# A two-layer block on one core: x through DRAM between stages, y summed by accumulating transfers, the feed-forward's activations split by GpSimd

## The chip, the cores and the metric

The kernel runs on one core of a Trainium2 chip. The metric is the device time of one execution in microseconds (us), median of three runs. The engines are TensorE (PE; its weight loads are PEld), VectorE (DVE), ScalarE (ACT), GpSimd (POOL) and SyncE (SP, which issues the transfers).

## The reference

Eight sequences of 512 tokens of width 256 pass through two layers, in float32. Each layer modulates a layernorm by per-sequence rows (`sa, ca, ga, sb, cb, gb`), adds a gated mixer and then a gated feed-forward. Cut to what matters:

```python
# layer 0: attention over features, then a shared and a routed feed-forward
h = layernorm(x) * (1 + ca) + sa
n = layernorm(h) * ln_g + ln_b
v, gate = split(silu(n @ W_hidden + b_hidden));  qk = silu(n @ W_qk + b_qk)
sim = einsum('bid,biD->bdD', qk * gamma0 + beta0, qk * gamma1 + beta1) / 512
x = x + ga * ((v * sum(softmax(sim), -1)[:, None] * gate) @ W_out + b_out + h)
h = layernorm(x) * (1 + cb) + sb
s = sigmoid(h @ router_w.T)          # the best 2 of 8 by s + bias, gates s / sum
x = x + gb * (silu(h @ sw1) * (h @ sw3) @ sw2 + sum_e comb_e * (gelu(h @ ew1[e]) @ ew2[e]))

# layer 1: a selective scan over time (512 channels, 16 states), then a ternary feed-forward
raw, gate = split(layernorm_mod(x) @ W_in)
h = silu(causal_conv4(raw));  ts, Bm, C = split(h @ W_x);  dt = softplus(ts @ W_dt + b_dt)
state[t] = exp(dt * A) * state[t - 1] + dt * Bm[t] * h[t]     # per channel and state d
y = sum_d state * C + h * D
x = x + ga * ((y * silu(gate)) @ W_out)
h = silu(tlin(x', w1)) * tlin(x', w2)          # tlin: ternary weights, then a scale per output
x = x + gb * tlin(gelu(tlin(gelu(tlin(h, h1)), h2)), w3)
```

## The kernel before

The work of one sequence (a "batch" b, eight in all) is four stages, each a Python generator that records operations: `front` (layer 0's mixer), `experts` (its feed-forward), `mixer` (the scan) and `ffn`. Activations lie with 128 tokens or 128 features on the partitions; most operations are 128x512 or 128x1024. Nothing is emitted while recording. Each operation carries its engine, an assumed cost, the buffers it reads and writes, and a due time: batch b's stage starts at b * TURN plus an offset, and a `lead` (RUSH, SLOW, EARLY) pulls an operation forward. `Plan.order` then plays a list scheduler over the assumed costs: at each moment an engine takes the ready operation with the earliest due time, if its buffers can be had from their pools, if it isn't more than AHEAD past the earliest open one, and (ScalarE) with LOOK added where the activation table would have to change. What comes out is one fixed order for each engine's queue, so a wait of one instruction holds up all that stand behind it on that engine.

Before all that, while the first batch's `front` runs, the kernel tests whether the feed-forward's weights are exact in the reduced format fp32r (`test`). With these inputs they are, and the branch that then runs multiplies in fp32r: an activation a is split into a high part rounded to fp32r and a low part a - high, and each weight meets both (`by`), so that a 128x512 product of one weight tile is two fp32r matmuls. Names used below:

- `st`, `v`, `decay`, `bp`, `crow`, `y`: the scan. For each state d and each half h of the channels (32 units u a batch) ScalarE writes exp(dt * A) to one of three `decay` buffers (L841), VectorE forms v = hs * B (L858) and scans 1024 wide over two chunks of 512 at once (L861; column 0 of each chunk of `decay` stays zero, which resets the state), GpSimd multiplies by C (L864) and adds to y (L866).
- `put` and the block after `gated`: the splits. ScalarE evaluates the activation twice, into the high part and back into PSUM (L991, L944), and VectorE subtracts (L915). For the first product of the feed-forward VectorE multiplies (L964), ScalarE casts (L971), VectorE subtracts (L973).
- `x_0` to `x_2`: x stays in SBUF from a batch's load to its `ffn`; three batches are held at once. `ffn` stores it to DRAM (`x_d`) and adds it back at the end through `xo`.
- `routing`: the scores take a sigmoid on ScalarE (L544), then some twenty small VectorE operations.
- matmul outputs: `ps_nT, ps_qk, ps_sim, ps_hv, ps_hg, pa_o` belong to front; `ps_hT, pg, pv, ps_r, pa_s, ps_e, pa_e` to experts; `ps_hTm, ps_raw, ps_x, ps_dt, ps_g, pa_m` to mixer; `ps_hTf, pg1, pv1, ps_h_s, pa_f, ps_o` to ffn (h1 and h2 are its two 1024x1024 products, a1 their first input).

## Time and profile before

| | us |
|---|---|
| median of 3 runs | 2246.09 (2244.88 to 2247.49) |
| the profiled execution, device time | 2246.68 |
| its span, first to last instruction | 2244.9 |
| busy in it: TensorE, ScalarE, VectorE, GpSimd | 1973.9, 1691.8, 1635.1, 1535.7 |
| mean granted TensorE clock | 0.94 of full speed |
| first product of the scan of batch 0, of batch 7 | 283.5, 1958.2 |
| last addition to y of batch 7, start | 2110.7 |

A row of the profile names the source line, the engine, the operation, the tiles written and read, the shapes and the count; then the busy time and the mean of one in ns; then how long the engine stood idle just before such instructions and who released it. The line of a matmul is that of a helper (L343), so matmuls are told apart by tiles. A window row gives busy time of each engine in a stretch of the execution. The span has a start of some 280 us in which the pipeline of batches fills, a middle that repeats every 243 us, and an end from 1958 on in which the last batch's scan and then its feed-forward run with little or nothing beside them.

### The profile page before, as it was taken

What the parts mean: (1) busy time and instruction counts of PE and PEld (TensorE: products, weight loads), DVE (VectorE), ACT (ScalarE), POOL (GpSimd) and SP (SyncE); (2) the same over time, 40 slices, a digit from 0 to 9 for tenths busy, and PEclk for the clock granted to TensorE, in tenths of its full rate; (3) what the DMA queues carried; (4) which work ended last, traced back from release to release, by engine and by line L of the source; (5) the groups of instructions that cost most, each with busy time, mean ns of one, the idle gap of its engine ahead of it and who ended that gap; (6) DMA issues with size and microseconds to landing.
All of it is one profiled execution on the core that took longest, in us unless ns stands there. A gap on an engine that the chain in (4) does not pass through costs nothing.

```text
span 2244.9 us, 22011 instructions
## 1 busy us (share of the span) xinstructions
PE 1973.9 (88%) x6916; PEld 1292.8 (58%) x6916; DVE 1635.1 (73%) x2074; ACT 1691.8 (75%) x2433; POOL 1535.7 (68%) x765
## 2 busy tenths in 40 slices
PE   1897879498999899999999999999999999768587
PEld 0455336245775567656765577656765677445465
DVE  4532589869885898669895998679876988598531
ACT  3522768569987898788988898789988898779442
POOL 1201488969896788567895789678876789399700
PEclk6998889699999999999999999999999999979888
DMA  9226335223453345334443345334533443335333
GB/s 264 77 93 191 88 108 167 79 91 122 142 175 106 112 133 171 112 111 139 158 157 117 115 150 174 116 118 140 170 121 117 140 150 116 120 108 169 103 104 105
DMA packets 186608, 294.52 MB, mean 131 GB/s; under 512 B 14232, under 2 KB 109728, under 8 KB 186480
## 3 DMA queue, kind: packets, MB, share of 16 engines
q1 hardware_dynamic: 186480, 293.01, 41.3%
q8 instruction: 57, 0.93, 0.2%
q14 instruction: 71, 0.58, 0.1%
HBM read 283.94 MB, written 20.55 MB: 136 GB/s over the span
## 4 chain that ended last, share of the span: by engine, by line
PE 67%; POOL 10%; ACT 9%; DVE 9%; issue 3%; DMA 1%; SPq 0%; DVEq 0%; POOLq 0%; ACTq 0%
PE ps_h_s L343 17%; PE pa_e L343 9%; PE ps_e L343 9%; PE ps_sim L343 4%; POOL st L864 4%; POOL y L866 4%; PE pg L343 4%; DVE st L861 3%; PE pv L343 3%; PE pa_m L343 3%; PE ps_qk L343 2%; PE pa_f L343 2%; PE ps_g L343 2%; PE pa_o L343 2%; PE pa_s L343 2%
## 5 line engine op out<-in xcount | busy, mean ns | idle before, releaser
L864 POOL TENSOR_TENSOR st<-st,crow 128x1024 f32<-128x1024 f32 x256 | 608.5, 2377 | 167.4 <-DVE st L861 103.0
L866 POOL TENSOR_TENSOR y<-y,st 128x1024 f32<-128x1024 f32 x256 | 607.7, 2374 | 18.1
L861 DVE TENSOR_TENSOR_SCAN st<-decay,v 128x1024 f32<-128x1024 f32 x256 | 584.6, 2284 | 35.7 <-POOL y L866 17.4
L841 ACT ACTIVATE decay<-dt,neg_a 128x511 f32<-128x511 f32 x512 | 335.8, 713 | 46.5 <-DVE st L861 41.3
L858 DVE TENSOR_TENSOR v<-hs,bp 128x1024 f32<-128x1024 f32 x256 | 313.3, 1224 | 13.6 <-ACT bp L853 8.6
L343 PE MATMUL ps_h_s<-a_h_sh,w_f_h 128*128 128x512 f32 x512 | 212.0, 414 | 35.3 <-DVE a_h_sl L915 31.7
L343 PE MATMUL ps_h_s<-a1h,w_f_h 128*128 128x512 f32 x512 | 220.5, 431 | 16.0 <-DVE a1l L973 14.7
L343 PE MATMUL pa_e<-w_e,ge 128*128 128x256 f32 x1024 | 232.1, 379 | 1.4 <-ACT ge L735 1.4
L343 PE MATMUL ps_e<-hT,w_e 128*128 128x512 f32 x512 | 231.4, 592 | 0.0
L343 PEld LDWEIGHTS pa_e<-w_e,ge 128*128 128x128 f32 x1024 | 194.4, 190 | 44.6 <-issue 15.3
L343 PE MATMUL ps_h_s<-a_h_sl,w_f_h 128*128 128x512 f32 x512 | 204.8, 400 | 0.0
L343 PE MATMUL ps_h_s<-a1l,w_f_h 128*128 128x512 f32 x512 | 202.8, 396 | 0.0
L841 ACT ACT_TABLE_LOAD x146 | 187.3, 1283 | 4.0 <-DVE st L861 1.3
L746 DVE SCALAR_TENSOR_TENSOR acc<-pa_e,rt,acc 128x256 f32<-128x256 f32 x256 | 112.0, 477 | 87.3 <-PE pa_e L343 86.3
L991 ACT ACTIVATE a_h_sh<-ps_h_s,cols 128x512 fp32r<-128x512 f32 x128 | 88.0, 688 | 110.4 <-PE ps_h_s L343 109.4
L915 DVE TENSOR_TENSOR a_h_sl<-ps_h_s,a_h_sh 128x512 fp32r<-128x512 f32 x128 | 87.4, 683 | 96.1 <-ACT ps_h_s L991 95.6
L343 PEld LDWEIGHTS ps_e<-hT,w_e 128*128 128x128 f32 x512 | 97.2, 190 | 92.4 <-issue 79.4
L343 PEld LDWEIGHTS ps_h_s<-a_h_sh,w_f_h 128*128 128x128 f32 x512 | 99.0, 193 | 70.4 <-DVE a_h_sl L915 35.7
L343 PEld LDWEIGHTS ps_h_s<-a1h,w_f_h 128*128 128x128 f32 x512 | 97.9, 191 | 48.9 <-DVE a1l L973 15.5
L735 ACT ACTIVATE ge<-ps_e 128x512 f32<-128x512 f32 x128 | 73.8, 598 | 54.1 <-PE ps_e L343 53.5
L343 PEld LDWEIGHTS ps_h_s<-a1l,w_f_h 128*128 128x128 f32 x512 | 97.9, 191 | 28.0 <-issue 8.7
L343 PE MATMUL ps_sim<-k,q 128*128 128x512 f32 x256 | 113.8, 603 | 0.0
(212 smaller groups left out, 3821.4 us busy)
## 6 DMA issues: line engine op xcount, KB each, us to landing
w_f_h<-fw_d SPq DMA_DIRECT2D x128, 512.0 KB, 3.5
w_e<-in_ew SPq DMA_DIRECT2D x128, 256.0 KB, 3.0
brow<-bc_d SPq DMA_DIRECT2D x128, 256.0 KB, 3.7
crow<-bc_d SPq DMA_DIRECT2D x128, 256.0 KB, 3.9
w_f<-fw_d SPq DMA_DIRECT2D x48, 512.0 KB, 4.0
w_s<-in_sw SPq DMA_DIRECT2D x24, 512.0 KB, 5.6
test<-in_f_h SPq DMA_DIRECT2D x16, 512.0 KB, 7.3
fw_d<-in_f_h SPq DMA_DIRECT2D x16, 512.0 KB, 6.4
```

The lines of the kernel that those rows point to most:

```text
L343: T.matmul(ps, lhsT=lhsT, rhs=rhs, start=(i == 0), stop=(i == last))
L735: op("ACT", 0.63, lambda ps=ps, g=ge[m]: A.activation(g.t, ps.t, AF.Gelu), r=[ps], w=[ge[m]], table="gelu", lead=RUSH)
L746: op("DVE", 0.48, lambda ps=ps, n=n, i=i, e=e: V.scalar_tensor_tensor(acc.t[:, n, :], ps.t[:, i * D : (i + 1) * D], comb(n, e), acc.t[:, n ...
L841: A.activation(decay[v % len(decay)].t[:, i, 1:], dt.t[:, c, 1:], AF.Exp, scale=neg_a.t[:, c, d : d + 1])
L858: op("DVE", 1.22, lambda v=v, cs=cs, bp=bp: V.tensor_tensor(v.t, hs.t[:, cs, :], over_tokens(bp.t, 2), ALU.mult), r=[hs, bp], w=[v])
L861: op("DVE", 2.28, lambda v=v, st=st, da=da: V.tensor_tensor_scan(st.t.rearrange("p c t -> p (c t)"), da.t.rearrange("p c t -> p (c t)"), v ...
L864: op("POOL", 2.4, lambda st=st, cc=cc: G.tensor_tensor(st.t, st.t, over_tokens(cc.t, 2), ALU.mult), r=[cc], w=[st])
L866: op("POOL", 2.4, lambda st=st, cs=cs: G.tensor_tensor(y.t[:, cs, :], y.t[:, cs, :], st.t, ALU.add), r=[st], w=[(y, pair(h))])
L915: op("DVE", 0.69, lambda: V.tensor_tensor(lo.t[:, at, :], ps.t, hi.t[:, at, :].bitcast(F32), ALU.subtract), r=[ps, (hi, at)], w=[(lo, at)] ...
L991: put(ps, nxt, m, lambda o, ps=ps, m=m, s=s: A.activation(o, ps.t, AF.Gelu, scale=col(s)[:, m : m + 1]), 0.69, [cols], table="gelu")
```

## The change

The scan: `decay` goes. ScalarE writes the exponentials straight into one of six `st` buffers, VectorE scans in place in two halves of 512, GpSimd multiplies by C, and y is summed by a transfer that GpSimd issues and that adds st to y. The feed-forward: an activation is evaluated once, into a float32 buffer (pool `two`, now six), and GpSimd makes the high part by a copy and the low part by a subtract (`split`). x: `experts` writes the new x to `x_d` in DRAM; `mixer` and `ffn` load it into `xn` and normalise it there, `mixer` loads it again in halves (`xm`), adds and stores it; two x buffers remain in SBUF. The router's sigmoid becomes exp, add and reciprocal. Four products reserve their results' buffers earlier (`need`). The planner's costs and due times change, with a separate turn for mixer and ffn; it also models the accumulating transfers, and lifts the AHEAD limit where nothing could be placed. The diff leaves out the planner's code and the `need` lines.

```diff
-TURN, FRONT, EXPERTS = 235.0, 64.0, 124.5
-MIX_AT, MIX = 221.7, 270.0
-FFN_AT, FFN = 531.0, 249.5
-FROM, UNTIL = 0.12, 0.949
-LOOK = 16.226
-DECAYS, BURST = 3, 1
-EARLY, RUSH, SLOW, AHEAD = 19.951, 14.0, 4.404, 69.662
+TURN, FRONT, EXPERTS = 206.087, 81.52, 133.488
+TURN_M, MIX_AT, MIX = 206.525, 229.452, 231.828
+TURN_F, FFN_AT, FFN = 208.187, 522.925, 195.397
+FROM, UNTIL = 0.218, 0.96
+LOOK = 38.649
+EARLY, RUSH, SLOW, AHEAD = 33.753, 17.315, -21.661, 137.531
...
-"two": (5, True), "bsc": (1, True), "bga": (1, True), "bgb": (1, True), "hs": (1, True),
-"dt": (1, True), "y": (1, True), "sp": (1, True), "st": (2, True), "bcb": (1, True),
+"two": (6, True), "bsc": (1, True), "bga": (1, True), "bgb": (1, True), "hs": (1, True),
+"dt": (1, True), "y": (1, True), "sp": (1, True), "st": (6, True), "bcb": (1, True),
...
-    op("ACT", 0.2, lambda: A.activation(at(SC, n), at(SC, n), AF.Sigmoid), w=[ps],
-       table="sigmoid", lead=RUSH)
+    op("ACT", 0.2, lambda: A.activation(at(SC, n), at(SC, n), AF.Exp, scale=-1.0), w=[ps],
+       table="exp", lead=RUSH)
+    v(0.2, lambda: V.tensor_scalar(at(SC, n), at(SC, n), 1.0, None, ALU.add))
+    v(0.2, lambda: V.reciprocal(at(SC, n), at(SC, n)))
...
-    op("POOL", 2.4, lambda: G.tensor_tensor(x.t, x.t, acc.t, ALU.add), r=[acc], w=[x], lead=RUSH)
-def mixer(b, x):
+    op("POOL", 2.4, lambda: G.tensor_tensor(acc.t, acc.t, x.t, ALU.add), r=[x], w=[acc], lead=RUSH)
+    op("SP", 1.7, lambda: SP.dma_start(out=x_d[b].t, in_=acc.t), r=[acc], w=[(x_d[b], (0, 1))], lat=2.0,
+       lead=RUSH)
+def mixer(b):
-    layernorm(x, xn, f"m{b}", RUSH)
+    load(xn, 512, lambda: SP.dma_start(out=xn.t, in_=x_d[b].t), r=[(x_d[b], (0, 1))])
+    layernorm(xn, xn, f"m{b}", RUSH)
...
-    def exps(u):
-        for v in range(u, u + BURST):
-            d, h = v // 2, v % 2
-            for i in range(2):
-                c = 2 * h + i
-                A.activation(decay[v % len(decay)].t[:, i, 1:], dt.t[:, c, 1:], AF.Exp,
-                             scale=neg_a.t[:, c, d : d + 1])
+    def exps(u, st):
+        d, h = u // 2, u % 2
+        for i in range(2):
+            c = 2 * h + i
+            A.activation(st.t[:, i, :], dt.t[:, c, :], AF.Exp, scale=neg_a.t[:, c, d : d + 1])
+    def scans(v, st):
+        for i in range(2):
+            V.tensor_tensor_scan(st.t[:, i, :], st.t[:, i, :], v.t[:, i, :], 0.0, ALU.mult, ALU.add)
-        da, cs = decay[u % len(decay)], slice(2 * h, 2 * h + 2)
+        cs = slice(2 * h, 2 * h + 2)
...
             op("ACT", 0.6, lambda bb=bb, bp=bp: A.copy(bp.t, bb.t), r=[bb], w=[bp], lead=SLOW)
-        if u % BURST == 0:
-            op("ACT", 1.42 * BURST, lambda u=u: exps(u), r=[dt, neg_a],
-               w=[decay[v % len(decay)] for v in range(u, u + BURST)], table="exp", lead=SLOW)
+        st = buf("st", [P, 2, S], f"st_{b}_{d}_{h}")
+        op("ACT", 1.42, lambda u=u, st=st: exps(u, st), r=[dt, neg_a], w=[st], table="exp", lead=SLOW)
-        st = buf("st", [P, 2, S], f"st_{b}_{d}_{h}")
-        op("DVE", 2.28, lambda v=v, st=st, da=da: V.tensor_tensor_scan(
-            st.t.rearrange("p c t -> p (c t)"), da.t.rearrange("p c t -> p (c t)"),
-            v.t.rearrange("p c t -> p (c t)"), 0.0, ALU.mult, ALU.add), r=[da, v], w=[st])
+        op("DVE", 2.35, lambda v=v, st=st: scans(v, st), r=[v], w=[st])
-        op("POOL", 2.4, lambda st=st, cs=cs: G.tensor_tensor(
-            y.t[:, cs, :], y.t[:, cs, :], st.t, ALU.add), r=[st], w=[(y, pair(h))])
+        op("POOL", 0.88, lambda st=st, cs=cs: G.dma_start(
+            out=y.t[:, cs, :], in_=st.t, accum_op=ALU.add), r=[st], w=[(y, pair(h))], move=2.8, lat=3.0)
...
-        add_gated(x, j, ps, ga, lambda: ga.t, f"tmpm_{b}_{j}")
-def ffn(b, x):
+        tmp, xo = buf("two", [P, 2, D], f"tmpm_{b}_{j}", line="tmp"), buf("two", [P, 2, D], f"xm_{b}_{j}", line="xm")
+        js = slice(2 * j, 2 * j + 2)
+        load(xo, 256, lambda xo=xo, js=js: SP.dma_start(out=xo.t, in_=x_d[b].t[:, js, :]),
+             r=[(x_d[b], j), (y, 0)], lead=RUSH, need=[tmp])
+        op("DVE", 0.69, lambda ps=ps, tmp=tmp: V.tensor_tensor(
+            tmp.t, ps.t.rearrange("p (i d) -> p i d", i=2), over_tokens(ga.t, 2), ALU.mult),
+            r=[ps, ga], w=[tmp], lead=RUSH)
+        op("POOL", 1.3, lambda tmp=tmp, xo=xo: G.tensor_tensor(tmp.t, tmp.t, xo.t, ALU.add),
+           r=[xo], w=[tmp], lead=RUSH)
+        op("SP", 1.4, lambda tmp=tmp, js=js: SP.dma_start(out=x_d[b].t[:, js, :], in_=tmp.t),
+           r=[tmp], w=[(x_d[b], j)], lat=2.0)
+def ffn(b):
     done, whole = 0.0, 80.0 if fast else 156.0
-    half = 0.5 if fast else 1.0
+    half = 0.53 if fast else 1.0
-    layernorm(x, xn, f"g{b}", RUSH)
-    op("SP", 2.7, lambda: SP.dma_start(out=x_d[b].t, in_=x.t), r=[x], w=[x_d[b]], lat=2.0)
+    load(xn, 512, lambda: SP.dma_start(out=xn.t, in_=x_d[b].t), r=[(x_d[b], (0, 1))])
+    layernorm(xn, xn, f"g{b}", RUSH)
...
-    def put(ps, a, k, fn, us, r, table=None):
-        hi, at = chunk(a, 0, k)
-        op("ACT", us, lambda: fn(hi.t[:, at, :]), r=[ps] + r, w=[(hi, at)], table=table, lead=RUSH)
+    def split(f, a, k):
+        (hi, at), (lo, _) = chunk(a, 0, k), chunk(a, 1, k)
+        op("POOL", 1.0, lambda: G.tensor_copy(hi.t[:, at, :], f.t), r=[f], w=[(hi, at)], lead=RUSH)
+        op("POOL", 1.3, lambda: G.tensor_tensor(
+            lo.t[:, at, :], f.t, hi.t[:, at, :].bitcast(F32), ALU.subtract),
+            r=[f, (hi, at)], w=[(lo, at)], lead=RUSH)
+    def put(ps, a, k, fn, us, r, name, table=None):
         if fast:
-            lo, _ = chunk(a, 1, k)
-            op("ACT", us, lambda: fn(ps.t), r=r, w=[ps], table=table, lead=RUSH)
-            op("DVE", 0.69, lambda: V.tensor_tensor(
-                lo.t[:, at, :], ps.t, hi.t[:, at, :].bitcast(F32), ALU.subtract),
-                r=[ps, (hi, at)], w=[(lo, at)], lead=RUSH)
+            f = buf("two", [P, S], name, line="split")
+            op("ACT", us, lambda: fn(f.t), r=[ps] + r, w=[f], table=table, lead=RUSH)
+            split(f, a, k)
+        else:
+            hi, at = chunk(a, 0, k)
+            op("ACT", us, lambda: fn(hi.t[:, at, :]), r=[ps] + r, w=[(hi, at)], table=table, lead=RUSH)
...
             if fast:
-                lo, _ = chunk(a, 1, m)
-                op("DVE", 0.745, lambda gated=gated, pv=pv: gated(pv.t), r=[sg, cols], w=[pv], lead=RUSH)
-                op("ACT", 0.62, lambda pv=pv, hi=hi, at=at: A.copy(hi.t[:, at, :], pv.t),
-                   r=[pv], w=[(hi, at)], lead=RUSH)
-                op("DVE", 0.69, lambda pv=pv, hi=hi, lo=lo, at=at: V.tensor_tensor(
-                    lo.t[:, at, :], pv.t, hi.t[:, at, :].bitcast(F32), ALU.subtract),
-                    r=[pv, (hi, at)], w=[(lo, at)], lead=RUSH)
+                f = buf("two", [P, S], f"f1_{b}_{m}", line="split")
+                op("DVE", 0.745, lambda gated=gated, f=f: gated(f.t), r=[pv, sg, cols], w=[f], lead=RUSH)
+                split(f, a, m)
...
-        load(xo, 256, lambda xo=xo, js=js: SP.dma_start(out=xo.t, in_=x_d[b].t[:, js, :]), r=[x_d[b]], lead=RUSH)
+        load(xo, 256, lambda xo=xo, js=js: SP.dma_start(out=xo.t, in_=x_d[b].t[:, js, :]),
+             r=[(x_d[b], j), fT[0]], lead=RUSH)
...
-slots_x = [fixed([P, NT, D], f"x_{i}") for i in range(3)]
-xs = [slots_x[b % 3] for b in range(B)]
+slots_x = [fixed([P, NT, D], f"x_{i}") for i in range(2)]
+xs = [slots_x[b % 2] for b in range(B)]
...
-    run(mixer(b, xs[b]), b * TURN + MIX_AT, MIX)
-    run(ffn(b, xs[b]), b * TURN + FFN_AT, FFN)
+    run(mixer(b), b * TURN_M + MIX_AT, MIX)
+    run(ffn(b), b * TURN_F + FFN_AT, FFN)
```

## The prediction, on record before the changed kernel ran

> A change of 0.2% (about 4.5 us) is what a measurement of this kernel can tell from none; the working below is in us.
>
> **What bounds the kernel now.** I read the page first, then the busy time in windows cut where each batch's scan begins (the first `st` product on GpSimd), then the groups and the chain of the last 300 us.
>
> ```profile
> PE 1973.9 (88%) x6916; PEld 1292.8 (58%) x6916; DVE 1635.1 (73%) x2074; ACT 1691.8 (75%) x2433; POOL 1535.7 (68%) x765
> ```
>
> The mean hides three regimes. Columns of the windows: stretch, length, busy PE, PEld, DVE, ACT, POOL, granted clock, DMA share, GB/s.
>
> ```profile
> 0.00:283.50 283.50, 201.48 (x576) 105.28 (x576) 120.53 (x254) 117.45 (x184) 61.80 (x54) 0.84 0.49 141
> 283.50:506.00 222.50, 168.57 (x493) 95.67 (x492) 176.56 (x216) 152.19 (x229) 190.78 (x95) 0.86 0.36 112
> 506.00:747.00 241.00, 232.30 (x836) 152.61 (x835) 196.32 (x249) 214.62 (x306) 191.35 (x93) 1.00 0.41 132
> ...
> 1241.00:1484.00 243.00, 236.30 (x858) 157.45 (x857) 199.91 (x251) 212.33 (x305) 190.60 (x95) 0.99 0.43 137
> ...
> 1958.20:2113.10 154.90, 101.64 (x349) 74.73 (x350) 129.58 (x98) 122.83 (x165) 151.00 (x64) 0.81 0.38 126
> 2113.10:2244.90 131.80, 108.31 (x435) 83.85 (x434) 30.56 (x50) 39.78 (x64) 3.76 (x5) 0.90 0.31 105
> ```
>
> In the middle TensorE is busy 236.3 of 243 per batch at clock 0.99: it is the bound, and nothing taken from another engine is worth more than the 6.7 left. In the first scan (283 to 506) and in the last (1958 to 2113) GpSimd is: 190.8 of 222.5 and 151.0 of 154.9, while TensorE waits at clock 0.86 and 0.81. The last stretch is one batch's feed-forward with nothing beside it. The rows that fill the scan, and those that the change touches:
>
> ```profile
> L864 POOL TENSOR_TENSOR st<-st,crow 128x1024 f32<-128x1024 f32 x256 | 608.5, 2377 | 167.4 <-DVE st L861 103.0 <-ACT ps_sim L643 38.1 <-DVE sums L646 26.2
> L866 POOL TENSOR_TENSOR y<-y,st 128x1024 f32<-128x1024 f32 x256 | 607.7, 2374 | 18.1
> L861 DVE TENSOR_TENSOR_SCAN st<-decay,v 128x1024 f32<-128x1024 f32 x256 | 584.6, 2284 | 35.7 <-POOL y L866 17.4 <-POOL st L864 0.8 <-DVE v L858 0.5
> L841 ACT ACT_TABLE_LOAD x146 | 187.3, 1283 | 4.0 <-DVE st L861 1.3
> L915 DVE TENSOR_TENSOR a_h_sl<-ps_h_s,a_h_sh 128x512 fp32r<-128x512 f32 x128 | 87.4, 683 | 96.1 <-ACT ps_h_s L991 95.6
> L991 ACT ACTIVATE ps_h_s<-ps_h_s,cols 128x512 f32<-128x512 f32 x128 | 83.6, 653 | 0.0
> L618 POOL TENSOR_TENSOR q<-q,gb_q 128x512 f32<-128x512 f32 x32 | 41.8, 1305 | 47.3 <-DVE q L616 34.5 <-PE pa_m L343 12.9
> L298 POOL MEMSET decay<- 128x1024 f32 x3 | 2.8, 951 | 0.0
> x_d<-x SPq DMA_DIRECT2D x8, 512.0 KB, 2.7
> ```
>
> **The change, engine by engine** (counts from the order of the two built programs, feed-forward branch that runs).
>
> GpSimd loses 256 adds into y: 256 x 2.374 = 607.7, and three memsets, 2.8. It gains 256 issues of accumulating transfers and 208 splits (26 a batch: 2 hT, 8 a1, 16 h), each a copy and a subtract. No row shows a DMA issued by GpSimd. Lower end 0.32, what SP takes to issue one; upper end 2.37, the add that it replaces. The Trainium skill (DMA: Bandwidth & Descriptors, Latency and other measured facts) puts the GpSimd path's first byte at about 1 us because software writes the descriptors; no row is near in kind, so I take 1.0. The copy: memset of 1024 took 951, so 0.48 at least, and at most 1.3 (two-input row L618); 1.0. The subtract: 1.3, same shape as L618. Sum: 256 + 208 x 2.3 = 734, net +124: 192 a batch becomes 207 (173 and 259 at the ends).
>
> VectorE loses 128 + 16 + 64 low-part subtracts, 140.7 in all; gains 16 small router operations (2.8) and runs each scan as two of half width. A half scan has no row; half of 2284 at least, plus up to 0.14 fixed (1224 for 1024 wide against 683 for 512), so 0 to 36; 18. Net -120: 204 to 189 a batch.
>
> ScalarE loses 144 second activations (83.6 for h, 11.9 for hT) and 64 casts (35.9), 131 in all. The longer LOOK should save table loads and the exp router removes 8 sigmoid loads, yet the order has 437 loads in the branch instead of 405. A row gives 1.283 each: +41. The skill (ScalarE: Activation LUTs, Table sets: the hidden batching unit) says to batch by set and counts about 2.7 per load: +86. The row decides; net -90 (-45 by the page), 211 to 200. Off the path in either case while TensorE is at 236.
>
> A rule that speaks against the change: the skill's GPSIMD Engine Reference, Engine selection, sends elementwise work on tiles to VectorE, GpSimd being about 2x slower with two inputs. The rows agree on the ratio (1305 against 683), but not on its meaning here. By the rule, the splits cost 478 on GpSimd in place of 272 on the other two, 206 more of engine time; by the windows, that time lies beside TensorE in the six middle turns and costs nothing until GpSimd nears 243. Where TensorE isn't the cover, in the last scan and tail, it costs in full, below.
>
> TensorE: the same matmuls, and 222 alternations between the two matmul kinds in both orders. x through DRAM: 6 more transfers a batch on SP (767 to 815 in all), 0.32 to 0.42 each to issue. Each xn load now waits on SP for a store's landing (2.7 by the x_d row), and the weight, brow and crow loads queued behind it wait too: up to 16 x 2.7 = 43 of blocked SP, hidden by weights loaded a block ahead; if that cover is gone, TensorE waits those 43. The accumulating transfers add 134 MB; at the rate of the page's 293 MB in 41.3% that is +19% of DMA time, at twice it (destination read too) +38%: 60 to 80%, not full. Each issue waits on GpSimd for the landing of the one two before; two units take 6.8, a 512 KB landing 2.7 to 4, so no stall; if landing took over 6.8, the products and splits behind it would wait. PSUM reservations (`need`) and the two-instead-of-three x buffers cost nothing: x is loaded a batch ahead.
>
> **The stages summed.** From the orders I priced what stands in each queue between one batch's scan start and the next. TensorE's matmuls are priced by the chain (start, length, records):
>
> ```profile
> 1449.15 6.87 PE ps_qk L343 x16
> ...
> 1565.19 3.68 PE ps_h_s L343 x16
> ```
>
> An f32 matmul leaves two records, so 8 of ps_qk take 0.859 each (256 wide: 0.43), and an fp32r one 0.229. Before, they add to 228.8 in a turn of 243: 14 of alternation and waits.
>
> - To scan 0: the order now puts the second batch's qk, hv, sim before the first mixer: 138 of matmuls before the last dt instead of 106; two waits (10.0 hTm, 5.5 dt) go. 283 becomes 292.
> - Scan 0 to 1: GpSimd 193 becomes 148; VectorE's 184 is now the largest. It took 223 with 30 over the largest; I take 16 over, 200.
> - Turns 1 to 7: matmuls 200, 226, 230, 226, 229, 210 in the new order, plus 13 (17 in the first: pa_o is followed by ps_hT at once, a wait of 10.4 before): 217, 239, 243, 239, 242, 223 against 241, 250, 244, 243, 243, 231.
> - Scan 7: GpSimd's queue holds 32 products (76), 32 issues (32), 22 splits of batch 6 (51): 160 + 2. It was 155; the saved adds are eaten by splits.
> - Tail: 132 becomes 142. Before, 13.3 (rest of pa_f, then pa_m) and 118.5 for the last feed-forward. Now two y products and pa_m, 8.3; then x is stored (2.7) and loaded (4.0) before the layernorm (+6.7), hT's two splits follow each other on GpSimd (+2), a1 is held to 2.3 a chunk against 1.83 of matmuls (+4), and the hand-overs after a1, h1 and h2 take 3.1 where two activations and a subtract took 2.05 (+3). 8.3 + 118.5 + 15.7 = 142.5.
>
> Sum: 292 + 200 + 217 + 239 + 243 + 239 + 242 + 223 + 162 + 142 = 2199 against 2244.9. The profiled run took 2246.68, 1.8 over its span, and stands 0.6 over the median 2246.09; 2199 + 1.2 gives 2200.
>
> **Rivals.**
> 1. GpSimd becomes the bound (slower). At 2.0 an issue its queue holds 230 to 249 a turn and 192 in scan 7: turns at 8 over that, where TensorE isn't longer, add 69, scan 7 adds 32: 2200 + 101 = 2301. It decides from about 1.75 an issue (or the same 24 a batch in dearer splits): 2245. At both upper ends (259 a turn, 210 in scan 7) about 2400. For: no row for either, in-order waits. Against: the page's 1 is well under 1.75. Chance 0.13.
> 2. The middle turns lose their idle 6.7 as well and the first scan runs at VectorE's 184: six turns x 7 and 13: 2145. For: VectorE and ScalarE have more room, and the new order puts other matmuls between h1 and h2. Chance 0.15.
> 3. The change doesn't do what it says at the start of stages: x's store and load (6.7) stand exposed ahead of each mixer: 8 x 6.7 = 54 gives 2254. For: TensorE's longest waits from 283 to 506 are just there:
>
> ```profile
> PE ps_hTm L462 <- ACT xn_m L451: 26.8, 1, 26.8
> PE ps_hT L462 <- ACT xn_f L451: 10.4, 1, 10.4
> ```
>
> Against: the new order puts sim ahead of hTm. Chance 0.12, half of it mild.
> 4. The forecast, 2160 to 2240: 0.60.
>
> Faster: 0.57 of the forecast, 0.15 and 0.05 of the third: 0.77. Same: 0.03 and 0.02. Slower: 0.13 and 0.05, 0.18. The range 2135 to 2270 leaves out about a tenth at the top (dear issues) and less below.
>
> **What would show it.** Right: scan 7 starts near 1895 (now 1958); GpSimd busy at 200 to 210 a turn; TensorE over 235 a turn; in the last scan GpSimd over 95% busy and the splits beside it; the wait of ps_hTm for xn_m (26.8) gone. Wrong: an issue row on GpSimd over 1.75, waits of GpSimd for DMA above 20 in all, a split over 2.8, or turns above 245 with TensorE waiting for a low part.

## The result, and the profile after

The changed kernel takes 2234.51 us (median of five runs, 2230.12 to 2237.73), the kernel before on the same chip 2245.72 (2240.05 to 2247.49): ratio 0.9953, 95% interval 0.9937 to 0.9969. It is faster by 11 us, a quarter of the 46 forecast. The profiled execution took 2237.6 us over a span of 2235.5, so it stands 3 above the median.

The busy times of the whole span, from the page:

```profile
PE 1969.3 (88%) x6916; PEld 1292.0 (58%) x6916; DVE 1520.0 (68%) x2138; ACT 1622.5 (73%) x2257; POOL 1547.7 (69%) x1178
```

Against the line of before: VectorE has 115 us less, ScalarE 69 less, GpSimd 12 more, TensorE 5 less. So VectorE and ScalarE were relieved nearly as forecast, and the time hardly followed. The windows, cut again where each batch's scan begins (stretch, length, busy PE, PEld, DVE, ACT, POOL, granted clock, DMA share, GB/s):

```profile
0.00:291.00 291.00, 211.37 (x636) 113.44 (x636) 129.84 (x273) 124.41 (x200) 61.08 (x55) 0.88 0.54 160
291.00:499.50 208.50, 162.52 (x482) 92.42 (x482) 174.46 (x241) 155.77 (x228) 142.58 (x93) 0.88 0.79 195
499.50:736.00 236.50, 223.24 (x774) 145.99 (x775) 181.18 (x253) 197.97 (x273) 184.18 (x136) 0.96 0.79 201
...
1468.00:1711.50 243.50, 237.42 (x860) 158.90 (x859) 183.65 (x260) 202.38 (x282) 192.91 (x146) 0.99 0.79 212
...
1938.00:2104.00 166.00, 99.72 (x334) 70.97 (x335) 118.94 (x113) 107.56 (x139) 147.25 (x112) 0.79 0.89 216
2104.00:2235.50 131.50, 111.10 (x460) 85.26 (x458) 12.84 (x24) 27.16 (x40) 58.45 (x63) 0.93 0.38 127
```

Four things are to be seen. The largest gain is in the first scan, 14 us, where GpSimd fell from 190.8 to 142.6 busy; half of it is given back by the later start of scan 0. In the middle TensorE's 237 stands over everything else, as before. In the last scan GpSimd is down to 89% busy and the stretch is longer than it was. From scan 0 to the end of the last scan the DMA share has doubled, to 0.8 and 0.9. Stage by stage, in us:

| stage | before | forecast | after | without transfers |
|---|---|---|---|---|
| to scan 0 | 283.5 | 292 | 291 | 291.4 |
| scan 0 to 1 | 222.5 | 200 | 208.5 | 202.4 |
| scan 1 to 2 | 241 | 217 | 236.5 | 232.1 |
| 2 to 3 | 250.5 | 239 | 245 | 241.9 |
| 3 to 4 | 243.5 | 243 | 248 | 247.5 |
| 4 to 5 | 243 | 239 | 239 | 238.0 |
| 5 to 6 | 243 | 242 | 243.5 | 241.1 |
| 6 to 7 | 231 | 223 | 226.5 | 223.1 |
| last scan and tail | 287 | 304 | 297.5 | 290.5 |
| span | 2244.9 | 2199 | 2235.5 | 2208.0 |

The last column is an experiment below. The rows that the change touched, from the groups (busy, mean ns of one, idle before and what ended it):

```profile
L879 POOL TENSOR_TENSOR st<-st,crow 128x1024 f32<-128x1024 f32 x256 | 648.8, 2551 | 92.6 <-DVE st L861 79.1 <-DVE ln_a L451 5.6 <-DVE more L573 2.9
L861 DVE TENSOR_TENSOR_SCAN st<-st,v 128x512 f32<-128x512 f32 x512 | 596.2, 1206 | 43.8 <-ACT st L856 21.0 <-POOL a_h_sl L937 8.4 <-DVE v L876 3.6
L881 POOL DMA_DIRECT2D y<-st x256 | 232.6, 915 | 48.2 <-POOL st L879 34.4 <-DMA y<-st 9.9 <-issue 1.8
L937 POOL TENSOR_TENSOR a_h_sl<-f_h_s,a_h_sh 128x512 fp32r<-128x512 f32 x128 | 164.0, 1281 | 10.3
L936 POOL CAST a_h_sh<-f_h_s 128x512 fp32r<-128x512 f32 x128 | 92.7, 725 | 70.5 <-ACT f_h_s L1020 70.4
```

An issue took 0.915 us on GpSimd, a copy 0.725, a subtract 1.281: all at or under what the prediction put. Two scan halves took 2.41 where one scan took 2.28. The queues, from the page (packets, MB, share of 16 engines' span; then KB each and us from issue to landing):

```profile
q1 hardware_dynamic: 193392, 309.79, 42.7%
q0 software_dynamic: 36864, 134.23, 32.2%
...
y<-st POOLq DMA_DIRECT2D x256, 512.0 KB, 6.4
w_f_h<-fw_d SPq DMA_DIRECT2D x128, 512.0 KB, 4.9
```

The accumulating transfers take 32.2% for 134 MB where the other queue takes 42.7% for 310 MB, 1.7 times as much per byte, and each lands after a median of 6.4 us, not after 2.7 to 4. The feed-forward's weight loads land after 4.9 us; without the transfers they take 3.5 (below).

TensorE's waits in the first scan, and the waits of all engines in the last (total, times, longest):

```profile
PE ps_nT L472 <- ACT xn_b L461: 15.7, 1, 15.7
PE ps_hT L472 <- ACT xn_f L461: 11.7, 1, 11.7
PE ps_hv L353 <- DMA w_hv<-in_W_hidden: 6.3, 1, 6.3
PE pa_e L353 <- ACT ge L747: 5.3, 1, 5.3
```

```profile
PE ps_h_s L353 <- ACT f_h_s L1020: 31.4, 14, 6.3
...
PE ps_hTf L973 <- ACT xn_g L461: 21.5, 1, 21.5
DVE y L892 <- DMA y<-st: 17.7, 1, 17.7
...
ACT st L856 <- DMA y<-st: 12.7, 4, 8.9
```

The wait of ps_hTm for xn_m (26.8) is gone, and the same 27 us stand under ps_nT and ps_hT: another layernorm of another batch is late next. In the last scan two waits carry the landing of the transfers into y, 17.7 where VectorE finishes y and 12.7 where ScalarE wants the state's buffer back.

### The profile page after: what moved, and what is told of

Same layout as the page of the kernel before. It is cut to its first block, busy times and chain, and to the rows that moved or that the text cites. A ratio compares the mean times of both kernels' runs of the same rounds, so it can differ in the third digit from the quotient of the medians.

```text
span 2235.5 us, 22822 instructions
## 1 busy us (share of the span) xinstructions
PE 1969.3 (88%) x6916; PEld 1292.0 (58%) x6916; DVE 1520.0 (68%) x2138; ACT 1622.5 (73%) x2257; POOL 1547.7 (69%) x1178
## 3 DMA queue, kind: packets, MB, share of 16 engines
q1 hardware_dynamic: 193392, 309.79, 42.7%
q0 software_dynamic: 36864, 134.23, 32.2%
## 5 line engine op out<-in xcount | busy, mean ns | idle before, releaser
L879 POOL TENSOR_TENSOR st<-st,crow 128x1024 f32<-128x1024 f32 x256 | 648.8, 2551 | 92.6 <-DVE st L861 79.1
L861 DVE TENSOR_TENSOR_SCAN st<-st,v 128x512 f32<-128x512 f32 x512 | 596.2, 1206 | 43.8 <-ACT st L856 21.0
L856 ACT ACTIVATE st<-dt,neg_a 128x512 f32<-128x512 f32 x512 | 336.8, 714 | 28.5 <-DMA y<-st 18.4
L881 POOL DMA_DIRECT2D y<-st x256 | 232.6, 915 | 48.2 <-POOL st L879 34.4
L937 POOL TENSOR_TENSOR a_h_sl<-f_h_s,a_h_sh 128x512 fp32r<-128x512 f32 x128 | 164.0, 1281 | 10.3
L1020 ACT ACTIVATE f_h_s<-ps_h_s,cols 128x512 f32<-128x512 f32 x128 | 87.9, 688 | 114.3 <-PE ps_h_s L353 103.0
L936 POOL CAST a_h_sh<-f_h_s 128x512 fp32r<-128x512 f32 x128 | 92.7, 725 | 70.5 <-ACT f_h_s L1020 70.4
```

The lines of the kernel that those rows point to most:

```text
L856: A.activation(st.t[:, i, :], dt.t[:, c, :], AF.Exp, scale=neg_a.t[:, c, d : d + 1])
L861: V.tensor_tensor_scan(st.t[:, i, :], st.t[:, i, :], v.t[:, i, :], 0.0, ALU.mult, ALU.add)
L879: op("POOL", 2.4, lambda st=st, cc=cc: G.tensor_tensor(st.t, st.t, over_tokens(cc.t, 2), ALU.mult), r=[cc], w=[st])
L881: op("POOL", 0.88, lambda st=st, cs=cs: G.dma_start(out=y.t[:, cs, :], in_=st.t, accum_op=ALU.add), r=[st], w=[(y, pair(h))], move=2.8, la ...
L936: op("POOL", 1.0, lambda: G.tensor_copy(hi.t[:, at, :], f.t), r=[f], w=[(hi, at)], lead=RUSH)
L937: op("POOL", 1.3, lambda: G.tensor_tensor(lo.t[:, at, :], f.t, hi.t[:, at, :].bitcast(F32), ALU.subtract), r=[f, (hi, at)], w=[(lo, at)], ...
```

## The experiments

The theories named in the expectations: **G**, the prediction's, that GpSimd's time binds the first and the last scan. **L**, that start and end are bound by one batch's chain of hand-overs and the middle by matmuls, so that GpSimd's time is worth little. **C**, that the gain was there and the transfers' traffic ate it. **M**, formed after the first runs, that relief and price simply add. Every kernel's time is set against runs of the kernel before on the same chip; a change of 0.2% can be told from none. "Against the changed kernel" is a ratio of two such ratios.

**1. The kernel before without the adds into y.**

```diff
-                op("POOL", 2.4, lambda st=st, cs=cs: G.tensor_tensor(
-                    y.t[:, cs, :], y.t[:, cs, :], st.t, ALU.add), r=[st], w=[(y, pair(h))])
+                op("POOL", 2.4, lambda: None, r=[st], w=[(y, pair(h))])
```

> The kernel before, with the 256 adds into y (GpSimd) issuing nothing; they keep their place in the plan, so the order of everything else stays. The output leaves out the states' sum in y. GpSimd loses 608 us. Theory G (the prediction's: GpSimd binds the first and the last scan): scan 0 to 1 falls from 222 to about 195 and scan 7 from 155 to about 135, so 2200 or less. Theory L (start and end are bound by one batch's own chain of hand-overs, the middle by matmuls, so GpSimd's time is nearly worthless): 2220 to 2240, TensorE's idle before scan 1 within 15 us of the 136 it had. Theory C (the change's gain was real and was lost to the DMA traffic of the accumulating transfers): as G, 2200 or less, because no transfer is added here.

Measured: 2234.72, ratio 0.9951 (0.9938 to 0.9964). 608 us off GpSimd are worth 10. The windows of the first and last scan of this kernel:

```profile
285.90:501.50 215.60, 165.28 (x492) 94.41 (x492) 176.15 (x216) 151.88 (x229) 116.66 (x63) 0.88 0.40 116
...
1950.10:2101.60 151.50, 101.16 (x346) 74.28 (x347) 130.31 (x100) 122.95 (x165) 76.10 (x32) 0.81 0.39 129
```

GpSimd's 151 in the last scan became 76, and the stretch fell by less than 5: in the runs the last scan is cut 6 us after its last product starts, and cut so the kernel before took 156.1 there, not 154.9. VectorE with 130 busy stood close behind GpSimd and had waits of its own. G falls, for this order of the queues; a new order for a GpSimd without adds was not tried. L got the number right; C's form "relief of GpSimd is worth 45 when no transfer is added" falls with G.

**2. The changed kernel without the accumulating transfers.**

```diff
-                op("POOL", 0.88, lambda st=st, cs=cs: G.dma_start(
-                    out=y.t[:, cs, :], in_=st.t, accum_op=ALU.add), r=[st], w=[(y, pair(h))], move=2.8, lat=3.0)
+                op("POOL", 0.88, lambda: None, r=[st], w=[(y, pair(h))], move=2.8, lat=3.0)
```

> The changed kernel, with the 256 accumulating transfers into y issuing nothing (they keep their place in the plan; the output leaves out the states' sum in y). GpSimd loses 233 us of issuing and the DMA queues 134 MB. Theory C (contention and landing waits ate the gain): 2205 or less, with the product on GpSimd back from 2.55 to 2.38. Theory L: at most 12 us off 2234, and those in the last scan, where y and st wait for landings.

Measured: 2209.70, ratio 0.9847 (0.9832 to 0.9862), 24 us under the changed kernel; the product is back at 2381 ns. By the table above, 6.1 of it lies in the first scan, 7 in the last scan and tail, and 14.8 in the six turns between. Most of it lies where L had nothing, and twice L's 12; C's number (2205 or less) is missed by 5. The transfers do cost what C says they cost, but not all of what was missing.

```profile
291.40:493.80 202.40, 161.16 (x481) 92.00 (x481) 174.28 (x241) 155.39 (x227) 114.14 (x61) 0.90 0.38 118
...
1917.50:2074.30 156.80, 95.54 (x321) 68.23 (x322) 119.83 (x115) 107.41 (x139) 119.11 (x81) 0.80 0.36 121
```

```profile
w_f_h<-fw_d SPq DMA_DIRECT2D x128, 512.0 KB, 3.5
```

The first two lines are windows, to be read against 208.5 and 166 of the changed kernel; the third is the landing of the weights, 4.9 with the transfers.

**3. The changed kernel with the old split.**

```diff
-                    f = buf("two", [P, S], name, line="split")
-                    op("ACT", us, lambda: fn(f.t), r=[ps] + r, w=[f], table=table, lead=RUSH)
-                    split(f, a, k)
+                    lo, _ = chunk(a, 1, k)
+                    op("ACT", us, lambda: fn(ps.t), r=r, w=[ps], table=table, lead=RUSH)
+                    op("DVE", 0.69, lambda: V.tensor_tensor(
+                        lo.t[:, at, :], ps.t, hi.t[:, at, :].bitcast(F32), ALU.subtract),
+                        r=[ps, (hi, at)], w=[(lo, at)], lead=RUSH)
```

(and for a1 the cast on ScalarE and the subtract on VectorE)

> The changed kernel with the split of the feed-forward's activations done as before (ScalarE evaluates twice or copies, VectorE subtracts) instead of by GpSimd. GpSimd loses 420 us, VectorE gains about 140, ScalarE about 130. Theory G: scan 7 is no longer held by GpSimd and falls from 165 to about 140, the tail from 132 by up to 9 (shorter hand-overs): 2200 to 2210. Theory L: only the hand-overs of the last feed-forward and part of scan 7 come back: 2218 to 2232. If instead VectorE's or ScalarE's load held the changed kernel's middle, the turns lengthen by 5 to 15 each: 2250 or more.

Measured: 2284.74, ratio 1.0172 (1.0159 to 1.0185), 50 over the changed kernel. Both G and L fail; the third outcome's number holds. The three turns between scans 3 and 6 take 257 to 262 with ScalarE at 216 to 222 and VectorE at 201 to 204 busy. The changed kernel needs the split on GpSimd as it stands, but the load alone doesn't explain the loss: the kernel before carried 212 and 200 in turns of 243. The transfers and an order planned with constants found for other operations (next experiment) may each have a part.

**4. The kernel before with the changed planning constants alone.**

```diff
-TURN, FRONT, EXPERTS = 235.0, 64.0, 124.5
+TURN, FRONT, EXPERTS = 206.087, 81.52, 133.488
...
```

(with the other constants, the load's 0.0032 per KB and half = 0.53)

> The kernel before with nothing but the changed kernel's planning constants (when each stage is due, look-ahead for table loads, leads, 0.0032 per KB of a load, half 0.53). No operation changes. If the gain of the changed kernel comes from the order (theory L would allow it: the start's chain is a matter of order): 2230 to 2240. If the constants only fit the changed operations: 2255 to 2290. Theory G says nothing on it beyond that GpSimd's 151 us in scan 7 stay: scan 7 at 150 or more.

Measured: 2310.13, ratio 1.0291 (1.0278 to 1.0305). The constants alone cost 65; they don't fit the operations of before. This bears on experiments 3, 5 to 8, 10, 12 and 15: they change operations or their costs, so the order is planned afresh with constants found for others, and part of what they lose may be that order. Experiments 1, 2, 9, 11, 13 and 14 keep the order of all that remains.

**5. The kernel before with the scan part alone.**

```diff
-        "dt": (1, True), "y": (1, True), "sp": (1, True), "st": (2, True), "bcb": (1, True),
+        "dt": (1, True), "y": (1, True), "sp": (1, True), "st": (5, True), "bcb": (1, True),
...
+                op("ACT", 1.42, lambda u=u, st=st: exps(u, st), r=[dt, neg_a], w=[st], table="exp", lead=SLOW)
...
+                op("DVE", 2.35, lambda v=v, st=st: scans(v, st), r=[v], w=[st])
...
-                op("POOL", 2.4, lambda st=st, cs=cs: G.tensor_tensor(
-                    y.t[:, cs, :], y.t[:, cs, :], st.t, ALU.add), r=[st], w=[(y, pair(h))])
+                op("POOL", 0.88, lambda st=st, cs=cs: G.dma_start(
+                    out=y.t[:, cs, :], in_=st.t, accum_op=ALU.add), r=[st], w=[(y, pair(h))], lat=5.8)
```

> The kernel before with the change's scan part alone: y summed by accumulating transfers, the decay written into the state's own buffer and each scan run as two halves (5 state buffers, which takes the room of 2 states and 3 decays). Split, router, x and constants stay as before. Theory M (the relief of GpSimd alone is worth the 10 us of the run without the adds, the transfers cost the 25 us of the run without the transfers): 2250 to 2265. Theory G (the relief of GpSimd, 375 us here, is what pays): 2225 or less. A third outcome, states held for landings starve the scans: 2300 or more, with the scan waiting for its buffer.

Measured: 2299.23, ratio 1.0222 (1.0206 to 1.0239). M's sum (2250 to 2265) fails by 34 and more, at the edge of the third outcome. That states held for landings starve the scans is not shown: from 700 to 1900 ScalarE's exp waited only 19.5 us for landings. GpSimd, with less to do, waited 259 us there for the scan of the next state, and over the whole run TensorE waited 47 us for transfers, against 14 before. Trading adds for transfers was a loss with the old split and the old constants.

**6. The kernel before with the split alone.**

```diff
-                    op("ACT", us, lambda: fn(ps.t), r=r, w=[ps], table=table, lead=RUSH)
-                    op("DVE", 0.69, lambda: V.tensor_tensor(
-                        lo.t[:, at, :], ps.t, hi.t[:, at, :].bitcast(F32), ALU.subtract),
-                        r=[ps, (hi, at)], w=[(lo, at)], lead=RUSH)
+                    f = buf("two", [P, S], name, line="split")
+                    op("ACT", us, lambda: fn(f.t), r=[ps] + r, w=[f], table=table, lead=RUSH)
+                    split(f, a, k)
```

(and the same for a1)

> The kernel before with the change's split alone: GpSimd makes the two parts of every feed-forward activation, ScalarE evaluates once, VectorE subtracts nothing; adds into y, router, x and constants as before. ScalarE loses 131 us, VectorE 141, GpSimd gains 420 and comes to about 244 us a batch. If GpSimd binds once it passes TensorE's 231 a turn: turns of 250 to 260, scan 7 at 190, 2330 to 2380. If what pays in the changed kernel is VectorE's and ScalarE's relief whatever GpSimd has: 2215 or less.

Measured: 2435.05, ratio 1.0827 (1.0813 to 1.0842), worse than the first outcome's range. Two windows, and the scan's row:

```profile
1312.00:1581.70 269.70, 247.33 (x858) 161.10 (x857) 184.01 (x225) 198.56 (x279) 239.95 (x146) 0.96 0.40 124
...
2106.10:2306.10 200.00, 105.99 (x343) 73.94 (x343) 116.84 (x74) 107.25 (x137) 195.40 (x114) 0.72 0.31 97
```

```profile
L861 DVE TENSOR_TENSOR_SCAN st<-decay,v 128x1024 f32<-128x1024 f32 x256 | 584.6, 2284 | 265.2 <-POOL y L866 248.6 <-ACT decay L841 10.8 <-POOL st L864 0.8
```

With GpSimd at 240 a turn, a turn takes 270, not 243 or 250: the scan waits 248.6 us for the add that frees the state, against 17.4 before; TensorE waits for what comes late through it, and its clock falls to 0.96. By these waits GpSimd does bind here, and at 97.7% of the last scan it binds there as well; what experiment 1 refutes is that it did so in the kernel before.

**7. The changed kernel with adds in place of transfers.**

```diff
-                op("POOL", 0.88, lambda st=st, cs=cs: G.dma_start(
-                    out=y.t[:, cs, :], in_=st.t, accum_op=ALU.add), r=[st], w=[(y, pair(h))], move=2.8, lat=3.0)
+                op("POOL", 2.4, lambda st=st, cs=cs: G.tensor_tensor(
+                    y.t[:, cs, :], y.t[:, cs, :], st.t, ALU.add), r=[st], w=[(y, pair(h))])
```

> The changed kernel with y summed by adds on GpSimd, as before, in place of the accumulating transfers; all else as changed. GpSimd goes from 193 to about 240 a turn, the DMA queues lose 134 MB. If the transfers are what makes the GpSimd split possible: turns of 250 and more, 2290 to 2350. If their contention costs what GpSimd's room gives (theory M with GpSimd not binding below 243): 2225 to 2245.

Measured: 2484.05, ratio 1.1054 (1.1039 to 1.1069). GpSimd has 238 to 246 in five turns of 269 to 286. Without the transfers the GpSimd split doesn't pay here.

**8. The changed kernel with one transfer for two states.**

```diff
+                if d % 2 == 0:
+                    kept[h] = st
+                else:
+                    even = kept[h]
+                    op("POOL", 2.4, lambda st=st, even=even: G.tensor_tensor(
+                        st.t, st.t, even.t, ALU.add), r=[even], w=[st])
+                    op("POOL", 0.88, lambda st=st, cs=cs: G.dma_start(
...
```

> The changed kernel with the states of two neighbouring d added on GpSimd first and one accumulating transfer for both: 128 transfers in place of 256, 67 MB less, GpSimd +23 us a batch (to about 216). Theory M (the transfers' traffic and landing waits cost 25 us, a wait or a share for each): 2215 to 2228. If their number doesn't matter, or GpSimd's 216 already slows the scans: 2234 or more.

Measured: 2368.59, ratio 1.0544 (1.0520 to 1.0567): 133 worse than the changed kernel for some 25 us more of GpSimd a turn and half the traffic. GpSimd stands at 216 to 220 in turns of 255 to 273. The pairs also hold a state's buffer longer, which this run doesn't take apart.

**9. Transfers of an eighth of the bytes.**

```diff
-                    out=y.t[:, cs, :], in_=st.t, accum_op=ALU.add), r=[st], w=[(y, pair(h))], move=2.8, lat=3.0)
+                    out=y.t[:, cs, :64], in_=st.t[:, :, :64], accum_op=ALU.add), r=[st], w=[(y, pair(h))], move=2.8, lat=3.0)
```

> The changed kernel with each accumulating transfer cut to 64 of its 512 columns (an eighth of the bytes, as many issues on GpSimd, as many rows; the output leaves out the other columns' state sums). If traffic and late landings cost the 25 us between the changed kernel and the one without transfers: 2208 to 2216. If the 233 us of issuing on GpSimd, and the order of GpSimd's queue, cost them: 2228 to 2236.

Measured: 2220.39, ratio 0.9886 (0.9871 to 0.9900), 15 us under the changed kernel and 9 over the one without transfers, each to within about 5: between the two outcomes. Its queue line and issue row:

```profile
q0 software_dynamic: 69632, 16.79, 9.2%
...
L881 POOL DMA_DIRECT2D y<-st x256 | 330.6, 1304 | 37.1 <-POOL st L879 36.7
```

The smaller transfers have more packets (272 each against 144), and cost GpSimd more, not less; still 15 us came back, and the weight loads land after 3.5 us again. So about 15 of the 24, or more, are bytes and landings; how the other 9 divide is not settled.

**10. The old split for the last two batches only.** 

```diff
+                if fast and b >= B - 2:
+                    lo, _ = chunk(a, 1, k)
+                    op("ACT", us, lambda: fn(hi.t[:, at, :]), r=[ps] + r, w=[(hi, at)], table=table, lead=RUSH)
+                    op("ACT", us, lambda: fn(ps.t), r=r, w=[ps], table=table, lead=RUSH)
...
-                if fast:
+                elif fast:
```

(and the same for a1)

> The changed kernel with before's split (ScalarE twice or a copy, VectorE subtracts) for the last two batches' feed-forward only, whose splits have no next batch's matmuls over them. If GpSimd's splits lengthen the last scan and the hand-overs of the tail, as the prediction's sum had it (162 and 142): 2215 to 2228. If the splits' place is worth nothing there, because VectorE is as near as GpSimd in the last scan: 2232 to 2240.

Measured: 2232.70, ratio 0.9947 (0.9930 to 0.9963): no difference from the changed kernel. Last scan and tail together take 299 against 297.5:

```profile
1930.70:2075.90 145.20, 79.11 (x240) 55.26 (x240) 127.01 (x129) 102.54 (x144) 104.80 (x66) 0.76 0.91 224
2075.90:2229.90 154.00, 134.29 (x552) 104.83 (x552) 36.99 (x60) 49.27 (x80) 3.80 (x4) 0.95 0.41 131
```

The scan ends earlier, at 145, but TensorE did 79 us of matmuls beside it instead of 100, and the rest stands in the tail. Who splits is worth nothing at the end, in the orders tried.

**11. The kernel before without low parts.**

```diff
-                    op("ACT", us, lambda: fn(ps.t), r=r, w=[ps], table=table, lead=RUSH)
-                    op("DVE", 0.69, lambda: V.tensor_tensor(
-                        lo.t[:, at, :], ps.t, hi.t[:, at, :].bitcast(F32), ALU.subtract),
+                    op("ACT", us, lambda: None, r=r, w=[ps], table=table, lead=RUSH)
+                    op("DVE", 0.69, lambda: None,
...
-                return [(wv(k), a[i][k // 4].t[:, k % 4, :]) for k in range(n) for i in range(parts)]
+                return [(wv(k), a[0][k // 4].t[:, k % 4, :]) for k in range(n) for i in range(parts)]
```

> The kernel before with the low parts not made: their subtract on VectorE (208 of 0.68 us) and ScalarE's second evaluation (144 of 0.65) issue nothing but keep their place in the plan, and TensorE multiplies the high part twice, so its matmuls stay in number and kind (the output leaves out the low parts' products). VectorE loses 141 us, ScalarE 95, GpSimd nothing. If VectorE's and ScalarE's time is what the change buys: 2195 to 2215. If the middle is held by matmuls and start and end by chains (theory L): 2228 to 2240.

Measured: 2213.01, ratio 0.9854 (0.9842 to 0.9867): 33 us, where 608 off GpSimd brought 10. By the busy times VectorE lost 125 and ScalarE 82. It is inside the first outcome's range, and L falls here. The gain lies in the turns from scan 1 on, 2 to 5 us each, and 8 in the tail:

```profile
1229.00:1468.40 239.40, 235.64 (x857) 157.72 (x856) 183.30 (x224) 202.23 (x287) 191.54 (x94) 0.99 0.44 140
```

TensorE's idle in this turn is 3.8 against 6.7 before, though neither VectorE nor ScalarE had been the longest: they hand TensorE its operands. But this run does two things at once. It relieves the two engines, and it takes the low part out of each hand-over to TensorE. TensorE's longest waits for low parts before, and for high parts in this run:

```profile
PE ps_h_s L343 <- DVE a_h_sl L915: 32.2, 10, 12.4
PE pg L343 <- DVE hTl L915: 23.5, 7, 5.0
...
PE ps_h_s L343 <- ACT a_h_sh L989: 18.7, 4, 13.6
PE pg L343 <- ACT hTh L943: 8.0, 7, 1.6
```

With all such rows the waits for parts fall from 85 to 45 us; all of TensorE's waits together fall by 21 and its busy time by 13. How much of the 33 is relief and how much the shorter hand-over is not taken apart.

**12. Experiment 10, and every second unit of the last scan added by GpSimd.**

```diff
+                if b == B - 1 and u % 2:
+                    op("POOL", 2.4, lambda st=st, cs=cs: G.tensor_tensor(
+                        y.t[:, cs, :], y.t[:, cs, :], st.t, ALU.add), r=[st], w=[(y, pair(h))])
+                else:
```

> As the kernel with the old split for the last two batches, and in the last batch's scan every second unit is added into y by GpSimd instead of by a transfer, so that fewer landings stand in line when y is read. If late landings at the end of the last scan cost the 10 us that the run without transfers gained there: 5 to 10 less than the kernel with the late old split alone, 2208 to 2222. If not: no difference from it.

Measured: 2224.73, ratio 0.9908 (0.9891 to 0.9925). It is 8 us under experiment 10 and 10 under the changed kernel, with intervals that don't overlap: this version beats both kernels. With GpSimd free of splits in the last scan (128.7 of 146 busy) half the transfers can go, and the waits of all engines for their landing in that stretch fall from 24 us in experiment 10 to 6.

**13. The changed kernel without low parts.** 

```diff
-                op("POOL", 1.3, lambda: G.tensor_tensor(
-                    lo.t[:, at, :], f.t, hi.t[:, at, :].bitcast(F32), ALU.subtract),
+                op("POOL", 1.3, lambda: None,
...
-                return [(wv(k), a[i][k // 4].t[:, k % 4, :]) for k in range(n) for i in range(parts)]
+                return [(wv(k), a[0][k // 4].t[:, k % 4, :]) for k in range(n) for i in range(parts)]
```

> The changed kernel with the low parts not made: GpSimd's 208 subtracts (1.28 us each, 266 in all) issue nothing but keep their place in the plan, and TensorE multiplies the high part twice (the output leaves out the low parts' products). If GpSimd's time is nearly free in the changed kernel, as it was in the kernel before without its adds (10 us for 608): 2226 to 2234. If GpSimd's splits now stand in the hand-overs between matmuls: 2205 to 2222.

Measured: 2227.38, ratio 0.9923 (0.9911 to 0.9936), 7 us for 263 us of GpSimd, in the first outcome's range. The subtracts are nearly as well hidden in the middle as forecast; the copies stayed.

**14. The kernel before without adds and without low parts** (experiments 1 and 11 together).

> The kernel before with both: no adds into y (GpSimd -608) and no low parts (VectorE -141, ScalarE -95, high part multiplied twice); the output leaves out both. It asks what relieving all three engines at no price at all is worth. If the two gains add: 2245 - 10 - 33 = 2202. If each engine stood behind the other, so that taking both frees more: 2190 or less. If a common floor of matmuls and chains is met: 2208 or more.

Measured: 2186.77, ratio 0.9728 (0.9714 to 0.9741): 60 us, not 10 + 33. No floor is met at 2200, and the gains more than add. The last scan shows how:

```profile
1927.80:2064.40 136.60, 100.94 (x360) 73.81 (x361) 116.22 (x74) 112.55 (x147) 76.25 (x32) 0.84 0.43 143
```

Cut alike, it took 156 before, 151.5 without adds, 154.5 without low parts, and 136.6 without both: in the last scan GpSimd on one side, VectorE and ScalarE with their hand-overs on the other, each stood behind the other. They don't slow each other by running at the same time: in the kernel before a scan took a median of 2287 ns in the 184 cases in which GpSimd computed beside it for over nine tenths of it, and 2278 in the 27 in which it did so for less than one tenth.

**15. The changed kernel with x kept in place and the sigmoid router** 

```diff
-            op("POOL", 2.4, lambda: G.tensor_tensor(acc.t, acc.t, x.t, ALU.add), r=[x], w=[acc], lead=RUSH)
-            op("SP", 1.7, lambda: SP.dma_start(out=x_d[b].t, in_=acc.t), r=[acc], w=[(x_d[b], (0, 1))], lat=2.0,
-               lead=RUSH)
+            op("POOL", 2.4, lambda: G.tensor_tensor(x.t, x.t, acc.t, ALU.add), r=[acc], w=[x], lead=RUSH)
...
-        slots_x = [fixed([P, NT, D], f"x_{i}") for i in range(2)]
+        slots_x = [fixed([P, NT, D], f"x_{i}") for i in range(3)]
```

(three x buffers leave 5 states and 5 small buffers; the new `need` of the three products and of the load of xm went back too)

> The changed kernel without the passage of x through DRAM between stages and with the sigmoid router: scan part, split and planning constants as changed, x in three buffers as before, which leaves room for 5 states and 5 small buffers in place of 6 and 6. If x's store and load lie exposed ahead of each mixer (the prediction's third rival): 2215 or less. If they are hidden and the room is worth nothing: 2230 to 2240. If the sixth state buffer is what the change of x pays for (transfers hold their state until they land): 2248 to 2275.

Measured: 2255.48, ratio 1.0048 (1.0032 to 1.0064), 21 over the changed kernel, in the third outcome's range. The prediction's third rival falls: the change of x pays in this setting, and in the changed kernel VectorE waits only 7.8 us in all for the load of xn_m and TensorE never for ps_hTm. That x pays by the sixth state buffer is not shown: ScalarE's st waits 18.2 us for landings here and 18.4 in the changed kernel. What rises is TensorE's wait for the parts of hT, from 7 to 29, which come through the small buffers. The router and `need` went with it.

## Why the prediction was wrong

The direction and the range held; the size was off by 34.5: 2200 forecast, 2234.5 measured (2199 and 2235.5 as spans). That the direction held was in part luck. The sum took its gain mainly from the first scan, by GpSimd's relief, and from fewer matmuls in the turn after it; relief of GpSimd is worth 10 by itself (experiment 1), and the second gain was for the most part a wrong count. The 162 for the last scan, near the 166 measured, was luck too: it was GpSimd's queue without a pause, and GpSimd was busy for 147; without transfers the stretch is 157.

None of the signs of being wrong that the prediction named showed: an issue took 0.915 (1.75), GpSimd waited 12 us for DMA in all (20), a split took 2.0 (2.8), and TensorE waited 2.8 us in all for low parts. They watched GpSimd; the miss lay in other places.

**The costs in the sum were mostly right.** Issue 0.915 (1.0 put), subtract 1.281 (1.3), VectorE -115 (-120), ScalarE -69 (-90). The copy was 0.64 to 0.73 (1.0). GpSimd came out at +12, not +124, for the most part because the splits take 412 us instead of 478 and because the next instruction begins some 0.6 us after an issue, under its record, as the timeline of GpSimd shows (start, length):

```profile
1301.34 0.88 POOL L881 DMA_DIRECT2D y<-st  x1 [0.30 <-POOL st L879]
1301.95 2.67 POOL L879 TENSOR_TENSOR st<-st,crow 128x1024 f32<-128x1024 f32 x1
```

All in, a transfer costs GpSimd 0.89 us (1547.7 less 1320.3 without transfers, over 256), near the 1 us that the prediction took from the Trainium skill (DMA: Bandwidth & Descriptors, Latency and other measured facts), though that figure is a time to the first byte and not an engine's busy time. The first rival, dear issues, did not come about. The rule that was weighed against the change (the Trainium skill, GPSIMD Engine Reference, Engine selection: elementwise work on tiles belongs on VectorE) has the speed right to a factor of about two (a subtract takes 1281 ns there and 683 on VectorE) but doesn't settle the choice: where GpSimd holds the adds, the split there costs 190 us (experiment 6), where it doesn't, taking it back to VectorE and ScalarE costs 50 (experiment 3), both without new constants.

**Step 1 that failed: the landing wait was put at none, the DMA share "60 to 80%, not full" at no cost.** The share was right, 0.8 in the turns and 0.89 in the last scan. But transfers landed after 6.4 us, weights 1.4 later than without them, and experiment 2 prices the whole at 24 us of device time (27.5 on the spans). Of these 27.5, TensorE's waits for DMA make 12 (34.7 against 22.9 without the transfers), its other waits 8 and its own busy time 8. The largest of the rows, in the changed kernel and without the transfers:

```profile
PE ps_h_s L353 <- DMA w_f_h<-fw_d: 12.6, 9, 3.9
PE ps_h_s L353 <- DMA w_f_h<-fw_d: 5.6, 7, 1.7
```

The 2.7 to 4 for a landing were those of plain transfers at a DMA share of 0.4.

**Step 2: the matmuls of turn 1 to 2, "200".** TensorE's busy time there is 223, with the transfers and without. Priced at what records of the same kind took in the middle turns of before, the 774 records of that turn are an estimated 218, so 200 was short by 18; the other 5 go with the clock of 0.96. The full turns were short too: the prediction priced 228.8 of matmuls in a turn of 243 where its own window had TensorE busy for 236.3, so half of the "14 of alternation and waits" were matmuls. Where the count went wrong is not on record. Without the transfers the turn still takes 232.1 against 217 forecast: 15 of the miss.

**Step 3: GpSimd as the bound of the first and last scan.** Experiment 1 refutes it, in the order of before: with 74 off GpSimd the first scan falls by 7 and the last by less than 5. 97% busy in the last did not show that it would shrink with GpSimd; experiment 14 shows that VectorE and ScalarE had to be relieved as well. The first scan stays at 217 even then. In the first scan the change did relieve GpSimd by 48, and the stretch fell by 14: what remained in TensorE's waits was 15.7 of nT and 11.7 of hT behind layernorms, as with the 26.8 of hTm before, which the prediction took to be gone for good. 8.5 of the miss, 6.1 of it the transfers'.

**Step 4, the other way: last scan and tail were put at 304 and took 297.5**, 7 of which are the transfers'. The lengthening by splits was overstated; by experiment 10 it makes no difference there who splits. (The prediction's parts of the last scan, 76 + 32 + 51, are 159 and not 160.)

On the spans, by the table: 27.5 from the transfers, 15 from the miscount, 7.5 from the smaller stages together and -13.5 at the end make 36.5.

**What the change buys and pays, as the runs leave it.** With neither adds nor transfers the changed kernel is 34 us faster than the kernel before (experiment 2), and the transfers take 24 of that back. The 34 is not taken apart. GpSimd's relief alone is worth 10 in the old order. Relief of VectorE and ScalarE with a shorter hand-over is worth 33 (experiment 11), but there 207 us of busy time go, here 184, and here the low part is still made. TensorE's waits for the parts of the feed-forward's activations fall from 85 us before to about 49 in the changed kernel, as the profile assigns them; its waits for DMA rise by 20. GpSimd has no room for the splits beside the adds, so the adds had to leave it, and the room for the states that the transfers hold comes from x. With the constants as they were, each part alone costs 50 to 190 (experiments 4 to 6), and taking either out of the whole costs 50 (3) or 250 (7); whether new constants would bring some of that back is not shown. That the two kernels lie within 11 us is the small difference of large terms.

Left open: how the 9 us between experiments 2 and 9 divide between GpSimd's time and late landings, what the 34 consists of, and the shares of the router, of `need` and of the state buffers.

## What to carry to other kernels

When several engines stand close together in a stretch, relieving one of them can bring next to nothing and relieving several more than the sum (10, 33, and 60 together): ask of each what its consumers wait for, rather than which is fullest, and try the relief alone, at no price, before building the replacement. Work moved to transfers is not free when it goes beside weight loads: price its traffic by what it does to the landing of the loads that TensorE waits for. Check a count of a queue against the busy time in the same window before resting a stage on it; here 228.8 stood against 236.3 in a window that the prediction itself shows.
